# A two-layer graph network on one core: the order of the prelude's loads and checks, and the last tile's gelus and the first norms between two gather passes

## The chip, the cores and the metric

The kernel runs on one core of a Trainium2 chip. The core has TensorE (PE) for matrix products, VectorE (DVE), ScalarE (ACT), GpSimd (POOL) and SyncE (SP); SP, ACT and POOL each have a queue of their own for issuing DMAs. The metric is the device time of one execution in microseconds, the median of the runs.

## The reference

There are 3,125 nodes with 256 features, and 103,125 edges (`src`, `dst`, and one of eight types for each), sorted by `dst`, with one loop at each node. Cut to what matters:

```python
xn = layernorm(x)
e = relu((xn[dst] - xn[src]) @ theta.T + theta_b + xn[src] @ phi.T + phi_b)
x = x + segment_max(e, dst) + mixer(xn)              # layer 0: pass 0 over the edges
xt = layernorm(x)
x = x + layernorm(xt + ffn_two_of_eight_experts(xt))  # experts picked from the mean of xt
xn = layernorm(x)
h_all = einsum('ni,rio->nro', xn, W)                  # eight relation tables of 256
agg = segment_sum(h_all[src, type], dst)              # layer 1: pass 1 over the edges
x = x + layernorm(gelu(agg + xn @ loop_w + h_bias + xn)) + linear_attention(xn)
x = x + moe_ffn_two_of_eight(layernorm(x))
```

Since xn[dst] @ theta doesn't depend on the source, the maximum over a node's edges is a maximum over rows of one table of nodes, `xn @ (phi - theta)`.

## The kernel before

The nodes lie in 25 tiles of 128 rows (3,200 with padding). They are sorted by degree, so that all nodes of a tile have nearly as many edges; a tile's edges are then gathered column by column, 128 rows of 1 KB for each GpSimd indirect DMA.

*Prelude.* The lists `dst_i`, `src_i`, `typ_i`, `nxt_i` (`dst` moved by one) come as tiles of 124 partitions of 832 integers, all from ACT's queue, and behind them the two matrices `th0` and `w_b`. The node features `x` come from SP's queue. DVE, POOL and PE follow an order that is written out by hand (`tc.manual_schedule`); ACT and the queues of SP and ACT are ordered by a scheduler. The steps, in the order of the code:

- `blk_f` takes each block's first `dst`; four transposes on PE and copies on ACT spread it (`firsts`). `signs_of` (ACT) and `counts_of` (DVE, L1029) count for each node how many blocks begin before it; `stretches_of` makes addresses of that, and POOL gathers a stretch (`row`) of 496 entries for each of seven groups of tiles (`QUADS`).
- `idx2` is src times 8 plus type, written to `e_idx` in DRAM.
- `bad` holds the checks that the edges are sorted and looped as expected (seven DVE instructions, L1124 to L1133). With a check of degrees they give `flag`, by which all engines branch to a fast or a general form.
- `place_signs_of` (ACT) and `places_of` (DVE, L1059) count within the stretch; this gives where each node's edges end, and `edges_of` has POOL gather the node's edge list (`raw`) from `e_idx`.
- From the degrees come `key`, the one-hot `hot`, its running counts (`all_`, `own`, `cum`), and `rank`, each node's place in the sorted order.
- `node_stats` and `node_table` normalize five tiles of x at a time, transpose them and write their rows of `btab`, the node table of pass 0. `last_rows` finishes the last tile.
- `hi_oh` and `lo_oh` are one-hots of the rank's two parts. 25 products of them on PE give `in_i` and `id_i`, the nodes in sorted order.
- `ntab` in DRAM takes x, the edge list and the degree of each node. `fetch` gathers one tile's rows of it (`nrow`) in sorted order and makes the tile's gather addresses `idx1`, `idx2g`.

*Pass 0* gathers rows of `btab` (L183, buffers `gt`), takes maxima on DVE, and runs all other work of the layer (mixer, norms, expert products) beside it as background jobs. The experts are guessed beforehand from a part of the tiles; `settle` (run as `routing`) finds the real ones at the end.

*Between the passes.* The last group of tiles (tile 0) ends pass 0: `hidden_products`, then eight gelus on ACT (`hidden_gelus`, L1437), the output products (`outputs_a`) and copies (`outputs_out`). Then comes a branch on `missed`, taken if the guess was wrong (here it isn't). After it a class `Four` handles up to four tiles at once: `mixed` (sum and statistics on DVE, a square root on ACT), `added` (normalize on DVE, times gamma and plus beta on POOL), `summed` (sum into x, statistics, a square root on ACT), `normed`. `table` transposes the result, makes eight relation rows of it with 16 matmul records, scatters them to `htab_f` in sorted order from POOL (L230) and writes them to `here` from SP. The steps of the next group are spread over the tables of the one before. Tiles are cut so:

```python
cuts = ((23, 24), (24, 25), (21, 23), (1, 5), (5, 9), (9, 13), (13, 17), (17, 21), (0, 1))
```

*Pass 1* gathers from `htab_f` and runs the rest of layer 1 beside it.

Of the kernel before, what the change touches and what calls it, by code (L numbers as in the profile page):

```python
# [11 lines left out]
F32 = mybir.dt.float32  # L12
BF16 = mybir.dt.bfloat16
I32 = mybir.dt.int32
AF = mybir.ActivationFunctionType
ALU = mybir.AluOpType
AX = mybir.AxisListType
# [63 lines left out]
def gps_kernel(ctx: ExitStack, tc: tile.TileContext, a, out):  # L81
# [20 lines left out]

    xin = a["x"]
    V.memset(x[:, NT - 1, :], 0.0)
    for g in range(4):
        nc.sync.dma_start(
            x[:, 5 * g : 5 * g + 5, :],
            xin[5 * g * P : (5 * g + 5) * P, :].rearrange("(t p) d -> p t d", p=P),
        )
    nc.sync.dma_start(x[:, 20:24, :], xin[20 * P : 24 * P, :].rearrange("(t p) d -> p t d", p=P))  # L110
    nc.sync.dma_start(x[:LAST, NT - 1, :], xin[24 * P : NN, :])
# [816 lines left out]
    with ExitStack() as prx:  # L928
# [8 lines left out]
        def list_load(name, ap):  # L937
            t = pre.tile([LP, LT], I32, name=name)
            S.dma_start(t, ap.rearrange("(p t) o -> p (t o)", t=LT))
            return t  # L940
# [3 lines left out]
        typ_i = list_load("typ_i", a["typ"])  # L944
        nxt_i = list_load("nxt_i", a["dst"][1 : EPAD + 1, :])
        th0 = mat_load("th0", a["th_T"], pre, D)
        w_b = mat_load("w_b", a["ph_T"], pre, D)
# [127 lines left out]

        V.tensor_copy(blk_f, dst_i[:, ::BLOCK])
        for j in range(LT // BLOCK):
            pt = ps_tr.tile([P, 2, P], F32, name="pt")
            PE.transpose(pt[:, 0, :LP], blk_f[:, j : j + 1].to_broadcast([LP, P]), ident[:LP, :LP])
            S.copy(firsts[:, j * LP : (j + 1) * LP], pt[:, 0, :LP])  # L1080
# [7 lines left out]
        nc.sync.dma_start(e_idx.rearrange("r w -> (r w)")[W : W + EPAD].rearrange("(p t) -> p t", t=LT), idx2)  # L1088
        V.tensor_scalar(blk_n[:, 4:], blk_n[:, 4:], 0.5, 0.5 * NB, op0=ALU.mult, op1=ALU.add)
        stretches_of(slice(4, 7))  # L1090
        real = pre.tile([P, NT], F32, name="real")
        V.tensor_scalar(real, dval, float(NN), None, op0=ALU.is_lt)
        en = pre.tile([P, 29], F32, name="en")
        V.memset(en[:, 0:1], 0.0)
        V.tensor_scalar(rev, io_f[:, :W], -1.0, float(W - 1), op0=ALU.mult, op1=ALU.add)
        zero = pre.tile([2, W], F32, name="zero")
        V.memset(zero, 0)
        nc.sync.dma_start(e_idx[0:1, :], zero[0:1, :])
        nc.sync.dma_start(e_idx[EPAD // W + 1 :, :], zero[1:2, :])
        for s in fives:  # L1100
            nc.sync.dma_start(
                ntab[P * s.start : P * s.stop, :D].rearrange("(t p) d -> p t d", p=P), x[:, s, :]
            )
        prv_row = pre.tile([P, P], F32, name="prv_row")
        V.memset(prv_row[:, 0:1], 0.0)
        V.tensor_copy(prv_row[:, 1:], ident[:, : P - 1])
        prv_col = pre.tile([P, P], F32, name="prv_col")
        V.memset(prv_col, 0.0)
        V.tensor_copy(prv_col[:, 0:1], ident[:, P - 1 : P])
        ones_b = pre.tile([P, P], BF16, name="ones_b")  # L1110
        V.memset(ones_b, 1.0)
        not_upto = pre.tile([P, P], BF16, name="not_upto")
        V.tensor_scalar(not_upto, upto, -1.0, None, op0=ALU.add)
        one_f = pre.tile([P, NV * NT], BF16, name="one_f")
        V.memset(one_f, 1.0)
        floor = pre.tile([P, 1], F32, name="floor")
        V.tensor_scalar(floor, pcol, LAST - 0.5, -0.5, op0=ALU.is_lt, op1=ALU.add)
        V.tensor_scalar(floor, floor, 2 * BIG, None, op0=ALU.mult)

        for q in (1, 3, 5):  # L1120
            place_signs_of(q)

        bad = pre.tile([P, 3], F32, name="bad")
        V.memset(bad, 0.0)  # L1124
        big = pre.tile([LP, LT], F32, name="big")
        own_e = pre.tile([LP, LT], F32, name="own_e")
        V.tensor_tensor(big, dst_i, nxt_i, op=ALU.is_gt)
        V.reduce_sum(bad[:LP, 1:2], big, axis=AX.X)
        V.tensor_scalar(bad[:LP, 1:2], bad[:LP, 1:2], float(1 << 17), None, op0=ALU.mult)
        V.tensor_tensor(own_e, src_i, dst_i, op=ALU.is_equal)  # L1130
        V.tensor_tensor(big, nxt_i, dst_i, op=ALU.is_gt)
        V.scalar_tensor_tensor(big, own_e, -1.0, big, op0=ALU.mult, op1=ALU.mult)
        V.reduce_sum(bad[:LP, 2:3], big, axis=AX.X)  # L1133
# [30 lines left out]
        hot_1 = hot.rearrange("p v t -> p (v t)")  # L1164
        all_ = pre.tile([P, NV * NT], F32, name="all_")
# [8 lines left out]
        for g in (2, 3, 4):  # L1174
            node_stats(fives[g])
            last_rows = node_table(fives[g])

# [12 lines left out]
        V.tensor_scalar(rank, rank, -1.0, None, op0=ALU.add)  # L1190

# [16 lines left out]
        val = pre.tile(sh, F32, name="val")  # L1208
        V.tensor_tensor(val, hi_oh, dval[:, :, None].to_broadcast(sh), op=ALU.mult)
# [12 lines left out]
        pi = ps_mm.tile([P, 512], F32, name="mm")  # L1222
        for t in range(NT):
            if t == 2:
                V.reduce_sum(bad[:, 0:1], pc[:, :3], axis=AX.X)
                V.tensor_scalar(flag, bad[0:1, 0:1], float(NN), 1e6, op0=ALU.add, op1=ALU.min)
            lo_oh = pre.tile([P, P], F32, name="lo_oh", bufs=6)
            V.tensor_scalar(lo_oh, io_f, lo_f[:, t : t + 1], None, op0=ALU.is_equal)
            PE.matmul(pi[:, :NT], lo_oh, val[:, t, :], start=(t == 0), stop=(t == NT - 1))
        last_rows()  # L1230

        V.tensor_scalar(in_i, pi[:, :NT], float(NN - 1), None, op0=ALU.min)
        V.tensor_copy(id_i, pi[:, :NT])
# [4 lines left out]
    def fast():  # L1238
# [183 lines left out]
        def hidden_products(ts, i):  # L1422

            at0 = ts[0] * P
            ph = ps_mm.tile([P, 512], F32, name="mm")
            for f in range(FC):
                for c in range(2):
                    PE.matmul(
                        ph[:, f * P : (f + 1) * P], w1[:, i, c, f * P : (f + 1) * P], xT[:, c, at0 : at0 + P],
                        start=(c == 0), stop=(c == 1),  # L1430
                    )
            return ph
# [6 lines left out]
        def outputs_a(ts):  # L1439
            for j, t in enumerate(ts):  # L1440
                py = pys[t] = pys[t] if t in pys else ps_mm.tile([P, 512], F32, name="mm")
                PE.matmul(py, ones_row, b2.rearrange("o i d -> o (i d)"), start=True, stop=True)
                for i in range(2):
                    for f in range(FC):
                        PE.matmul(  # L1445
                            py[:, i * D : (i + 1) * D], hTs[i][:, f, j * P : (j + 1) * P], w2[:, i, f, :],
                            start=False, stop=(f == FC - 1), skip_group_check=True,
                        )

        def outputs_out(ts):  # L1450

            for t in ts:
                py = pys.pop(t)
                if t == 0:
                    y1 = seconds[t] = seconds[t] if t in seconds else f0h.tile([P, D], F32, name="y1_0", bufs=1)
                else:
                    y1 = seconds[t] = f0h.tile([P, D], F32, name="y1", bufs=SECONDS)
                S.copy(xT[:, :, t * P : (t + 1) * P], py[:, :D].rearrange("p (c n) -> p c n", c=2))
                S.copy(y1, py[:, D:])
# [21 lines left out]
        with ExitStack() as l0x:  # L1481
# [34 lines left out]
            fetch(2)  # L1516
# [264 lines left out]
            with tc.manual_schedule(engines={ET.DVE, ET.Pool, ET.PE, ET.Activation}):  # L1781
                fin[0].sums(0)
                fin[0].norms()
                routing = settle()
                next(routing)
                ts = GROUPS[-1]
                phs = [hidden_products(ts, i) for i in range(2)]
                for _ in routing:
                    pass
                for i in range(2):  # L1790
                    hidden_gelus(ts, i, phs[i])
                outputs_a(ts)
                outputs_out(ts)

        again = nc.values_load(missed[0:1, 0:1])
        with tc.If(again > 0):
# [8 lines left out]
            for ts in GROUPS:  # L1805
# [9 lines left out]
                hidden(ts)  # L1815
                outputs_a(ts)
                outputs_out(ts)
                if ts != GROUPS[-1]:
                    outputs_b(ts)
# [4 lines left out]
        with ExitStack() as tx:  # L1824
# [88 lines left out]
            cuts = ((23, 24), (24, 25), (21, 23), (1, 5), (5, 9), (9, 13), (13, 17), (17, 21), (0, 1))  # L1913
            fours = [Four(range(a, b)) for a, b in cuts]
            for part_ in fours[0].steps():
                for job in part_:
                    job()
            for four, after in zip(fours, fours[1:] + [None]):
                steps = after.steps() if after is not None else []
                each = -(-len(steps) // four.k)  # L1920
# [472 lines left out]
```

## Time and profile before

| | |
|---|---|
| median of 3 runs | 2603.63 us (2600.09 to 2603.84) |
| profiled execution | 2603.32 us, its span 2601.6 us |
| PE, DVE, ACT, POOL busy | 1792, 1263, 561, 1772 us |
| mean granted TensorE clock | 0.83 |
| prelude, to the first gather of pass 0 | 0 to 111.8 us |
| pass 0, first to last gather | 111.8 to 1184.4 us |
| between the passes, to the first gather from `htab_f` | to 1433.9 us |
| pass 1 and the end | to 2601.6 us |

The first three rows give the time and one execution's parts; times within the profile count from the start of its span. A row of the timeline that is shown further on gives the start in us, the duration in us (of all instructions of the row together), the engine, the line of the code, the operation, what it writes and reads, and in brackets how long the engine had been idle before and what released it. ACTq and SPq are the issues of DMAs on those engines. In the names buffer numbers are left out, so `idx` is `idx2` at L1087 and `idx1` in the gathers of pass 0.

### The profile page before, as it was taken

To read this page: it belongs to the slowest core of one execution; us is meant where nothing else is said; L and a number is where in the kernel's file an instruction comes from. 1 tells how busy PE (TensorE), PEld (TensorE's weight loads), DVE (VectorE), ACT (ScalarE), POOL (GpSimd) and SP (SyncE) were. 2 spreads that over 40 slices of the span, in tenths; PEclk is the share of its full clock that TensorE was granted. 3 is DMA by queue.
4 is the path that set the end of the run, shared out by engine and by line. 5 is a ranking of instruction groups with operands and counts; after the bars stand their busy time and mean duration, and the time that the engine had idled before them with its cause. 6 is when DMAs were issued, how large, how long until landed. Compare 5 with 4: busy or idle time off the path is not lost.

```text
span 2601.6 us, 20970 instructions
## 1 busy us (share of the span) xinstructions
PE 1792.2 (69%) x6143; PEld 1072.0 (41%) x6143; DVE 1262.6 (49%) x3108; ACT 561.0 (22%) x1319; POOL 1772.0 (68%) x1850
## 2 busy tenths in 40 slices
PE   1646677306743623764897627597898989999998
PEld 1523344104422312442343416243343545766787
DVE  6654656337344343444653344543635464655542
ACT  3313331002110100121121312121212122333333
POOL 3577777777777777772443777777776777777760
PEclk9777888657967767876999859698899989999998
DMA  6533334334333333331677753333333333333330
GB/s 181 126 107 108 105 104 122 103 103 133 102 103 103 103 101 103 103 102 59 248 299 304 224 155 102 111 100 105 97 103 89 103 108 107 102 106 101 103 90 13
DMA packets 128464, 314.99 MB, mean 121 GB/s; under 512 B 38636, under 2 KB 63282, under 8 KB 121932
## 3 DMA queue, kind: packets, MB, share of 16 engines
q0 software_dynamic: 86784, 252.90, 32.9%
q1 hardware_dynamic: 36510, 56.37, 6.4%
q10 hardware_dynamic: 5038, 4.21, 0.6%
q8 instruction: 53, 0.87, 0.1%
q14 instruction: 79, 0.65, 0.1%
HBM read 246.65 MB, written 66.70 MB: 120 GB/s over the span
## 4 chain that ended last, share of the span: by engine, by line
PE 26%; POOL 9%; issue 8%; DVE 5%; DMA 4%; ACT 1%; DVEq 0%; POOLq 0%; ACTq 0%
POOL gt L183 9%; PE mm L2156 8%; PE py L2189 8%; PE mm L178 7%; DMA gt<-htab_f,idx2g 3%; DVE gt L1269 1%; PE pt L2166 1%; PE mm L2050 1%; PE mm L2125 1%; DVE bnst L152 1%; DMA htab_f<-hs,id_i 1%; DVE hT L2174 0%; DMA out_dram<-x,id_i 0%; DVE acc L1274 0%; DMA xn<-here,own_i 0%
## 5 line engine op out<-in xcount | busy, mean ns | idle before, releaser
L183 POOL DMA_INDIRECT gt<-htab_f,idx2g x814 | 800.2, 983 | 269.4 <-issue 219.3
L183 POOL DMA_INDIRECT gt<-btab,idx x814 | 796.9, 979 | 251.6 <-issue 221.5
L1269 DVE TENSOR_TENSOR gt<-gt 128x256 f32<-128x256 f32 (+1 forms) x831 | 445.5, 536 | 738.8 <-DMA gt<-btab,idx 477.3
L2189 PE MATMUL py<-hT,w 128*128 128x256 f32 (+4 forms) x1408 | 384.1, 431 | 49.9 <-DVE hT L2174 49.9
L2156 PE MATMUL mm<-xT,w 128*128 128x256 f32 (+4 forms) x1408 | 375.0, 419 | 12.7 <-DVE x L2056 10.3
L2189 PEld LDWEIGHTS py<-hT,w 128*128 128x128 f32 x1408 | 245.7, 202 | 183.8 <-issue 81.2
L2156 PEld LDWEIGHTS mm<-xT,w 128*128 128x128 f32 x1408 | 241.6, 199 | 137.9 <-issue 86.0
L2160 ACT ACTIVATE hT<-mm,b 128x256 f32<-128x256 f32 (+4 forms) x352 | 170.3, 495 | 413.1 <-PE mm L2156 404.4
L178 PE MATMUL pt<-w_own,xT 128*128 128x256 f32 x100 | 37.4, 504 | 262.7 <-DVE acc L1685 262.7
L2174 DVE TENSOR_TENSOR hT<-hT,pt 128x1024 f32<-128x1024 f32 (+4 forms) x88 | 117.5, 1335 | 169.8 <-PE pt L2166 169.8
L178 PE MATMUL mm<-w_rel,xT 128*128 128x512 f32 x400 | 180.1, 609 | 4.4 <-ACT xT L173 3.6
L1274 DVE TENSOR_TENSOR acc<-acc,gt 128x256 f32<-128x256 f32 x403 | 172.7, 429 | 13.9
L178 PEld LDWEIGHTS pt<-w_own,xT 128*128 128x128 f32 x100 | 22.9, 254 | 273.5 <-DVE acc L1685 267.7
L178 PEld LDWEIGHTS mm<-w_rel,xT 128*128 128x128 f32 x400 | 76.6, 195 | 99.9 <-issue 85.8
L1416 PE MATMUL mm<-xT,w 128*128 128x384 f32 (+2 forms) x320 | 95.6, 464 | 14.9 <-DMA w<-in_f_W_dram 14.9
L1702 PE MATMUL pmean<-ones,xt 128*128 128x1 f32 (+1 forms) x100 | 21.7, 321 | 121.2 <-DVE xt L161 121.2
L1692 ACT ACTIVATE rs<-rs 128x3 f32<-128x3 f32 (+2 forms) x11 | 2.2, 204 | 452.4 <-DVE rs L1691 452.4
L1445 PE MATMUL mm<-w,hT 128*128 128x256 f32 x400 | 93.0, 386 | 0.1
L230 POOL DMA_INDIRECT htab_f<-hs,id_i x25 | 24.8, 990 | 96.9 <-DMA htab_f<-hs,id_i 25.3
L178 PE MATMUL mm<-w_qkv,xT 128*128 128x512 f32 (+1 forms) x200 | 87.2, 553 | 0.5 <-ACT xT L173 0.5
L1445 PEld LDWEIGHTS mm<-w,hT 128*128 128x128 f32 x400 | 74.1, 190 | 28.1 <-issue 18.2
L1416 PEld LDWEIGHTS mm<-xT,w 128*128 128x128 f32 x320 | 63.6, 219 | 46.3 <-DMA w<-in_f_W_dram 15.3
(398 smaller groups left out, 2143.6 us busy)
## 6 DMA issues: line engine op xcount, KB each, us to landing
here<-hs SPq DMA_DIRECT2D x25, 1024.0 KB, 3.9
gt<-btab,idx POOLq DMA_INDIRECT x814, 2.8
gt<-htab_f,idx2g POOLq DMA_INDIRECT x814, 2.8
w<-in_f_W_dram SPq DMA_DIRECT2D x20, 512.0 KB, 9.3
ntab<-x SPq DMA_DIRECT2D x5, 640.0 KB, 10.2
btab<-bs SPq DMA_DIRECT2D x5, 640.0 KB, 3.9
otab<-xn SPq DMA_DIRECT2D x25, 128.0 KB, 1.7
acc<-otab SPq DMA_DIRECT2D x25, 128.0 KB, 2.2
```

The source lines that it names most:

```text
L152: V.bn_stats(out=st, in_=src)
L178: PE.matmul(ps, lhs[:, c, t * P : (t + 1) * P], w[:, c, :], start=start and c == 0, stop=stop and c == 1)
L183: G.indirect_dma_start(out=dst, out_offset=None, in_=table, in_offset=bass.IndirectOffsetOnAxis(ap=idx, axis=0))
L1269: V.tensor_tensor(gt[:, :h, :], gt[:, :h, :], gt[:, m - h : m, :], op=op)
L1274: V.tensor_tensor(acc, own(t) if i == 0 else acc, gt[:, 0, :], op=op)
L1416: PE.matmul(ph[:, :n], w1[:, i, c, f * P : (f + 1) * P], xT[:, c, at0 : at0 + n], start=(c == 0), stop=(c == 1),)
L1445: PE.matmul(py[:, i * D : (i + 1) * D], hTs[i][:, f, j * P : (j + 1) * P], w2[:, i, f, :], start=False, stop=(f == FC - 1), skip_group_che ...
L2050: PE.matmul(pa, ones_row, b_lu, start=False, stop=True)
L2156: PE.matmul(ph[:, :n], w1s[e][:, c, f * P : (f + 1) * P], xT[:, c, at0 : at0 + n], start=(c == 0), stop=(c == 1),)
L2160: S.activation(hT[:, f, :n], ph[:, :n], AF.Gelu, bias=b1[:, e, f : f + 1])
L2174: V.tensor_tensor(hT[:, :, :n], hT[:, :, :n], wb[:, None, :n].to_broadcast([P, FC, n]), op=ALU.mult)
L2189: PE.matmul(self.py[c][:, :n], w2s[e][:, f, c * P : (c + 1) * P], hT[:, f, :n], start=False, stop=(e == NX - 1 and f == FC - 1),)
```

## The change

In the prelude, the lists, x and the matrices are loaded in one written order from SP's queue; the writes to `e_idx` go to ACT's queue; small set-up operations move ahead; the checks `bad` move behind `hot`; `last_rows` moves ahead to behind `rank`; `in_i` is found from two bf16 digits of the node's number; and the `fits` to `flag` part moves behind `in_i`. One tile is fetched in full before the first gather, and the second only asked for. Between the passes, the last tile's gelus and outputs move from before the branch to after the first steps of two groups, and the cuts change.

```diff
-            S.dma_start(t, ap.rearrange("(p t) o -> p (t o)", t=LT))
+            nc.sync.dma_start(t, ap.rearrange("(p t) o -> p (t o)", t=LT))
             return t
 
         dst_i = list_load("dst_i", a["dst"][:EPAD, :])
         src_i = list_load("src_i", a["src"])
         typ_i = list_load("typ_i", a["typ"])
+        V.memset(x[:, NT - 1, :], 0.0)
+        node_load(slice(0, 5))
+        th0 = mat_load("th0", a["th_T"], pre, D, nc.sync)
+        w_b = mat_load("w_b", a["ph_T"], pre, D, nc.sync)
+        node_load(slice(5, 10))
         nxt_i = list_load("nxt_i", a["dst"][1 : EPAD + 1, :])
-        th0 = mat_load("th0", a["th_T"], pre, D)
-        w_b = mat_load("w_b", a["ph_T"], pre, D)
+        node_load(slice(10, 15))
+        node_load(slice(15, 20))
+        node_load(slice(20, 24))
+        nc.sync.dma_start(x[:LAST, NT - 1, :], a["x"][24 * P : NN, :])
...
-        nc.sync.dma_start(e_idx.rearrange("r w -> (r w)")[W : W + EPAD].rearrange("(p t) -> p t", t=LT), idx2)
+        S.dma_start(e_idx.rearrange("r w -> (r w)")[W : W + EPAD].rearrange("(p t) -> p t", t=LT), idx2)
...
         V.reduce_sum(rank, cum.rearrange("p (v t) -> p t v", t=NT), axis=AX.X)
         V.tensor_scalar(rank, rank, -1.0, None, op0=ALU.add)
+
+        last_rows()
...
-        val = pre.tile(sh, F32, name="val")
-        V.tensor_tensor(val, hi_oh, dval[:, :, None].to_broadcast(sh), op=ALU.mult)
+        vals = pre.tile([P, NT, 2, NT], BF16, name="vals")
+        for m in range(2):
+            V.tensor_tensor(vals[:, :, m, :], hi_oh, digits[:, m, :, None].to_broadcast(sh), op=ALU.mult)
+        pi = ps_mm.tile([P, 512], F32, name="mm")
+        for t in range(NT):
+            lo_oh = pre.tile([P, P], BF16, name="lo_oh", bufs=6)
+            V.tensor_scalar(lo_oh, io128, lo_f[:, t : t + 1], None, op0=ALU.is_equal)
+            PE.matmul(pi[:, : 2 * NT], lo_oh, vals[:, t, :, :].rearrange("p m t -> p (m t)"), start=(t == 0), stop=(t == NT - 1))
+        id_f = pre.tile([P, NT], F32, name="id_f")
+        V.tensor_copy(id_f, pi[:, NT : 2 * NT])
+        V.scalar_tensor_tensor(id_f, pi[:, :NT], 64.0, id_f, op0=ALU.mult, op1=ALU.add)
+        V.tensor_scalar(in_i, id_f, float(NN - 1), None, op0=ALU.min)
+        V.tensor_copy(id_i, id_f)
...
-        pi = ps_mm.tile([P, 512], F32, name="mm")
-        for t in range(NT):
-            if t == 2:
-                V.reduce_sum(bad[:, 0:1], pc[:, :3], axis=AX.X)
-                V.tensor_scalar(flag, bad[0:1, 0:1], float(NN), 1e6, op0=ALU.add, op1=ALU.min)
-            lo_oh = pre.tile([P, P], F32, name="lo_oh", bufs=6)
-            V.tensor_scalar(lo_oh, io_f, lo_f[:, t : t + 1], None, op0=ALU.is_equal)
-            PE.matmul(pi[:, :NT], lo_oh, val[:, t, :], start=(t == 0), stop=(t == NT - 1))
-        last_rows()
-
-        V.tensor_scalar(in_i, pi[:, :NT], float(NN - 1), None, op0=ALU.min)
-        V.tensor_copy(id_i, pi[:, :NT])
+        V.reduce_sum(bad[:, 0:1], pc[:, :3], axis=AX.X)
+        V.tensor_scalar(flag, bad[0:1, 0:1], float(NN), 1e6, op0=ALU.add, op1=ALU.min)
...
-            fetch(2)
+            ask(2)
+            fetch(1)
...
                 for _ in routing:
                     pass
-                for i in range(2):
-                    hidden_gelus(ts, i, phs[i])
-                outputs_a(ts)
-                outputs_out(ts)
...
-            cuts = ((23, 24), (24, 25), (21, 23), (1, 5), (5, 9), (9, 13), (13, 17), (17, 21), (0, 1))
+            cuts = ((23, 25), (20, 23), (1, 5), (5, 9), (9, 13), (13, 17), (17, 20), (0, 1))
             fours = [Four(range(a, b)) for a, b in cuts]
-            for part_ in fours[0].steps():
+
+            first, second = fours[0].steps(), fours[1].steps()
+            for part_ in (first[0], second[0], first[1], second[1], first[2], first[3]):
                 for job in part_:
                     job()
+            for i in range(2):
+                hidden_gelus(GROUPS[-1], i, phs[i])
+            outputs_a(GROUPS[-1])
+            outputs_out(GROUPS[-1])
             for four, after in zip(fours, fours[1:] + [None]):
                 steps = after.steps() if after is not None else []
+                if four is fours[0]:
+                    steps = second[2:]
```

Not shown: the seven lines of `bad` are the same at their new place; so are the set-up operations; the five writes `ntab<-x` stand behind the node tables in the code, and in the order of SP's queue behind all loads and ahead of the first write of `btab`. The digits are the node's number shifted right by six and its low six bits. The second half of the expert outputs of tile 0 has no buffer of its own any more (`y1_0`); in the branch that isn't taken here, the last group redoes its hidden products only. The orders within both passes are the same as before. In the scheduled order of ACT after the branch stand: four gelus, the square root of tiles 23 and 24, one gelu, that of tiles 20 to 22, three gelus, a copy of the outputs, and the square root of 23 and 24 in `summed`.

## The prediction

> **What bounds the kernel now.** I read busy time by stage first, then the rows of DVE and POOL up to the first gather of pass 0, then ACT, PE and POOL between the passes. A row of the first view gives a stretch in us and its length, busy us (instructions) of PE, PE's weight loads, DVE, ACT and POOL, the granted clock, the DMA share and GB/s.
>
> ```profile
> 0.00:112.00 112.00, 47.15 (x218) 38.03 (x218) 71.15 (x223) 47.91 (x125) 41.04 (x75) 0.87 0.58 148
> 112.00:1186.00 1074.00, 563.52 (x1822) 342.03 (x1822) 499.66 (x1285) 169.99 (x489) 818.67 (x837) 0.73 0.38 108
> 1186.00:1434.00 248.00, 203.63 (x514) 95.65 (x515) 124.66 (x342) 47.39 (x111) 85.12 (x99) 0.91 0.62 238
> ```
>
> The reader is to see that pass 0 (row 2) is POOL's: 837 gathers in 1074 us, each 0.95 busy and 0.30 issue. The prelude (row 1) and the stretch between the passes (row 3) have no engine full, save PE at 82% in the latter. The change edits only these two, 360 us; the orders of instructions inside both passes stay. So the answer is how much earlier each pass's first gather starts.
>
> The prelude is a chain of waits. DVE:
>
> ```profile
> 12.04 0.17 DVE L1076 CAST blk_f<-dst_i 124x4 f32<-124x4 int32 x1 [8.57 <-DMA dst_i<-in_dst_dram]
> ...
> 24.48 1.03 DVE L1087 SCALAR_TENSOR_TENSOR idx<-src_i,typ_i 124x832 f32<-124x832 int32 x1 [0.69 <-DMA typ_i<-in_typ_dram]
> ...
> 32.35 1.03 DVE L1127 TENSOR_TENSOR big<-dst_i,nxt_i 124x832 f32<-124x832 int32 x1 [3.25 <-DMA nxt_i<-in_dst_dram]
> ...
> 41.99 0.72 DVE L1059 TENSOR_SCALAR_CACHE_REDUCE junk<-row,dval 128x496 bf16<-128x496 int32 x1
> ...
> 94.59 0.14 DVE L1226 TENSOR_SCALAR flag<-bad 1x1 int32<-1x1 f32 x1
> ...
> 105.10 0.18 DVE L1232 TENSOR_SCALAR in_i<-mm 128x25 int32<-128x25 f32 x1 [1.88 <-PE mm L1229]
> ```
>
> DVE waits for lists at 12.0, 24.5 and 32.4; the counting of places (L1059) starts at 42.0 only because the checks of the edges and the first statistics stand before it; the branch's `flag` is ready 10.5 us before the node order `in_i`, so the branch is hidden. What is released then, on POOL:
>
> ```profile
> 105.55 0.94 POOL L183 DMA_INDIRECT nrow<-ntab,in_i  x1 [16.54 <-DVE id_i L1233]
> ...
> 111.83 0.96 POOL L183 DMA_INDIRECT gt<-btab,idx  x1 [3.90 <-ACT x L1513]
> ```
>
> Between the passes, ACT leaves the branch at 1209.76, and PE gets its tables in starts and stops:
>
> ```profile
> 1209.76 1.28 ACT L1849 ACT_TABLE_LOAD   x1 [2.80 <-ACTq L1796]
> 1216.07 0.66 PE L172 MATMUL pt<-ident,z 128*128 128x128 f32 x2 [9.79 <-DVE z L161]
> 1217.19 8.76 PE L178 MATMUL mm<-w_rel,xT 128*128 128x512 f32 x16 [0.46 <-ACT xT L173]
> 1227.87 0.44 PE L172 MATMUL pt<-ident,z 128*128 128x128 f32 x2 [1.92 <-DVE z L161]
> 1228.77 7.13 PE L178 MATMUL mm<-w_rel,xT 128*128 128x512 f32 x16 [0.46 <-ACT xT L173]
> 1240.96 1.08 PE L172 MATMUL pt<-ident,z 128*128 128x128 f32 x4 [5.06 <-DVE z L161]
> 1242.07 15.13 PE L178 MATMUL mm<-w_rel,xT 128*128 128x512 f32 x32
> ```
>
> One tile's 16 records take 7.3 us; tiles 23, 24 and 21/22 each wait for norms that were begun too late. From 1260.7 on PE runs without a gap. The scatters (L230) stand at 1228.1, 1240.6, 1257.6, 1263.3, and then 21 intervals, 163.4 us in all, to 1426.7; the first gather from the table is at 1433.85.
>
> **The prelude, step by step.** *Loads.* The lists went out on ACT's queue beside x on SP's. Their 3,328-byte packets passed at 13 to 17 per us while x ran, at 24 when x paused (22 to 24 us); 124 packets are 5.2 us alone. Now dst, src, typ, x's first five tiles, th0 and w_b stand in that order in one queue: dst at 2.5 (first packets) + 5.2 + 0.5 = 8.2, src 13.4, typ 18.6, the x tiles 20.5, w_b some 22. Here a rule speaks against the change. The Trainium skill, "DMA: Bandwidth & Descriptors", section "Issuing engines are not separate DMA queues", says that transfers share the same 16 engines whoever starts them, so several issuers save only issue time; read so, one queue changes nothing for dst (12.0), the firsts gain only ACT's own delay, the prelude would gain some 8 us, and the time be 2586. I take the rows: the packets did slow down beside x, and a queue orders what two queues mix.
>
> *Firsts.* ACT issued six loads and started its first table load (1.28) at 17.5, so the firsts ended at 20.1; now they end at 11.3. Seven row gathers (1.25 each) follow, hidden behind DVE's wait for typ: idx2 runs 18.7 to 19.7, node_stats 20.6 to 23.4, the w_b subtraction (0.69), places at 24.3 against 42.0: -17.7. The small set-up operations that moved lie in the waits for lists.
>
> *To `hot`.* The first five tiles' table now shares ACT with the place signs; a product of the degree stands behind it on PE: +2.1. `hot` ends at 47.2 against 62.8. The checks (seven operations, 6.2 us by L1127 to L1133) come here, before node_table(1): 53.4. Its first xT follows at 55.2 against 66.82: -11.6. From there the five-tile groups and the scan keep their pace (ACT some 1.09 us a tile): rank 77.6 against 89.2.
>
> *Order.* From rank to in_i before: 15.9 us (val 0.81, fits to bad 2.4, 25 one-hots of 0.36, PE's tail 1.9). Now: a wait for the last tile's product to 80.5 (last_rows stands first), then 3.6 us to the end of two digit products (0.81 each), 25 one-hots, which become bf16, at 0.18 (a 128x128 bf16 output, L1113, took 0.16; at the old 0.36 it would be 4.5 more), 25 bf16 products instead of 50 fp32 records of 0.22, and three short operations: in_i at 89.5, 11.9 us.
>
> *Flag.* It now comes last: 3.6 us of DVE and PE, 93.1. Then every engine's branch, which nothing hides any more. Before shows ACT issuing 3.2 us after flag, and at the later branch DVE after 1.0 and ACT after 2.8; for POOL it shows only an upper bound, 10.9 us (flag to nrow). I take 2.1, between DVE's and ACT's. nrow at 95.2: -10.3. One tile is fetched before the first gather instead of two: 4.3 us instead of 6.3. First gather 99.5 against 111.8: **-12** (7 if the branch costs POOL 7, 17 if the lists land at 4.1 us each and the branch costs 1).
>
> *Costed at nothing:* the write of e_idx, moved to ACT's queue, holds ACT until idx2 and a load have come, near 22; behind it stand the place signs, whose rows don't land before 21 to 23. It lands about 31, and the 25 raw gathers (1.25 each) run to some 68 instead of 89; only the nrow gathers at 95 want them. ntab and the node table move past each other on SP: ntab's five writes (3.2 MB, some 14 us at 230 GB/s) follow the last x load, which lands near 34, and end near 48; the first node-table write behind them must free its buffer for group 2 at 63.5, so 13 us cover it.
>
> **Between the passes.** The last tile's gelus leave the stretch before the branch, where they lay beside it: ACT goes to the branch at 1202.3 instead of 1207.0, and is through at 1205.3. But ACT's order there is now four gelus, sqrt, one gelu, sqrt, three gelus, a copy, sqrt: six table loads in place of one after the branch and one before it, 7.7 us. Following it: sqrt of 23/24 at 1209.1, sqrt of the next three at 1212.2, copy 1215.3, sqrt 1216.8, norm, transposes, first table at 1218.2, 1.0 later than before. The Trainium skill, "ScalarE: Activation LUTs", section "What ACT_TABLE_LOAD costs", puts a switch at 2.66 us, 1.28 of load and 1.38 of drain. By that the six cost 8.3 more and this part would bring 1 us. The trace has the exponential done at 1200.82, the load at 1200.84 for 1.28, the gelu at 1202.13, so no drain; I take 1.28.
>
> Then the five tiles stand ready together. Scatters after the first table: +10.9, +18.3, +31 (four tiles' multiplies on POOL, 1.55 us each, stand before the third), +36.7, against +10.9, +23.4, +40.4, +46.1. The 21 intervals after it are bound by PE and the 1 MB writes as before, less 0.7 for one lone tile fewer. So -9.4 + 1.0 - 0.7: **-9** (5 to 13). The second buffer y1 and the rare branch cost nothing: not taken, or an allocation.
>
> **Sum.** The profiled execution took 2603.3 (span 2601.6), within 0.3 of the median of 2603.6. 2603.3 - 12 - 9 = 2582.
>
> **The rivals.** (a) *Half is eaten.* POOL's branch costs up to its bound of 10.9 and the prelude brings 3; or the scatters are bound by their writes from the first on, so that an earlier table start brings 2. For it: scatters wait for DMA in the dense part at 7.5 us each. Against it: the first four lie 12.5 and 17 apart, with idle PE. 2591 to 2595. (b) *No gain.* Both of these at once, or the skill's table switch with the branch at its bound: 2599 to 2603. (c) *Slower:* SP's one queue. All loads, ntab's writes and the node table's now stand in it in turn, and lists use few of the 16 engines. If that backlog frees the node-table buffer after 63.5, each us goes one for one into rank and the first gather. It takes back the whole gain at 84.5 and decides from 90 on (0.2%): the loads and writes would have to take 87 us in place of some 50. At 95 it gives 2613. For it: ACT waited for a node-table write already (0.7 us at 87.85). Against it: DMA is at 58% in the prelude, raw gathers move few bytes.
>
> **How the numbers follow.** 0.2% is 5.2 us, about what a measurement of this kernel can tell from no change. Both gains as summed: 0.70 (2574 to 2592, time 2582). (a) 0.13, (b) 0.07, (c) 0.10. Faster 0.83, same 0.07, slower 0.10. The range 2569 to 2599 takes in the low ends of the bounds (-17 and -13 together give 2573) and all of (a); (c) and most of (b) are left out.
>
> **What would show it.** Right: blk_f near 8, idx2 near 19 waiting for typ_i, the first place count near 24, hot before 50, nrow near 95 with POOL's wait named after flag or the branch, first gather 98 to 101; after the branch six table loads of 1.28, first table 1217 to 1220, five tiles with no gap, the first gather of pass 1 some 21 us earlier; pass 0 from first gather to last (1073 us) and pass 1 to the end (1168) as before. Wrong: a place count after 35, a node-table wait over 5 us, a drain beside the table loads, or either pass longer by more than 5.

## The result, and the profile after

The changed kernel takes 2590.8 us (median of 4 runs, 2588.7 to 2593.9) against 2603.7 us (4 runs): ratio 0.9952, 95% interval 0.9935 to 0.9969. It is 12.9 us faster; 2582 was forecast. The profiled execution, the slowest of the four, took 2593.92 us; its span of 2592.2 us is 9.4 us less than that of before. The windows, in the order of columns told above:

```profile
0.00:112.00 112.00, 46.73 (x193) 33.62 (x193) 69.64 (x227) 47.47 (x125) 43.87 (x75) 0.84 0.55 153
112.00:1186.00 1074.00, 571.86 (x1822) 345.58 (x1822) 498.80 (x1288) 170.26 (x489) 818.22 (x836) 0.73 0.37 107
1186.00:1426.00 240.00, 204.57 (x515) 96.53 (x516) 124.76 (x338) 52.66 (x114) 85.66 (x99) 0.91 0.64 246
```

The stretch between the passes is 8 us shorter with the same work in it; the prelude is as long as it was. By the starts of the gathers:

| stretch, us | before | after | change | forecast |
|---|---|---|---|---|
| to the first gather of pass 0 | 111.83 | 110.80 | -1.0 | -12 |
| pass 0, first to last gather | 1072.6 | 1073.0 | +0.4 | 0 |
| last gather to the first from `htab_f` | 249.4 | 241.8 | -7.7 | -9 |
| from there to the end | 1167.8 | 1166.7 | -1.1 | 0 |

In the prelude, DVE's rows (lines are numbered anew) show the gain being made:

```profile
9.59 0.17 DVE L1098 CAST blk_f<-dst_i 124x4 f32<-124x4 int32 x1 [5.39 <-DMA dst_i<-in_dst_dram]
...
19.95 1.03 DVE L1119 SCALAR_TENSOR_TENSOR idx<-src_i,typ_i 124x832 f32<-124x832 int32 x1 [3.84 <-DMA typ_i<-in_typ_dram]
...
25.05 0.72 DVE L1060 TENSOR_SCALAR_CACHE_REDUCE junk<-row,dval 128x496 bf16<-128x496 int32 x1
...
91.62 0.18 DVE L1230 TENSOR_SCALAR in_i<-id_f 128x25 int32<-128x25 f32 x1
...
95.05 0.14 DVE L1245 TENSOR_SCALAR flag<-bad 1x1 int32<-1x1 f32 x1
```

The place counts start 17 us earlier and `in_i` is ready 13.5 us earlier. POOL's rows show where those went:

```profile
104.76 0.95 POOL L173 DMA_INDIRECT nrow<-ntab,in_i  x1 [28.04 <-DMA wr<-in_f_WrT_dram]
...
110.80 0.96 POOL L173 DMA_INDIRECT gt<-btab,idx  x1 [3.65 <-issue]
```

`nrow` comes 13.0 us after the order that it needs. 3.4 of that is the flag, which now comes last; the other 9.6, from 95.19 on, are POOL's way through the branch. In the kernel before, flag was ready at 94.73; with the same 9.6 POOL would have been ready at 104.3, just before `in_i` at 105.3. By this estimate the branch was hidden there with 1 us to spare (3 us with 7.6 us, the shortest of the cases below), and a faster `in_i` alone could bring no more than that.

Between the passes, ACT's rows show the six table loads:

```profile
1205.95 1.28 ACT L1449 ACT_TABLE_LOAD   x1 [5.82 <-PEq L1802]
1207.25 1.14 ACT L1449 ACTIVATE hT<-mm,b 128x128 f32<-128x128 f32 x4
1208.41 1.28 ACT L1858 ACT_TABLE_LOAD   x1
1209.70 0.20 ACT L1858 ACTIVATE rsz<-rsz 128x2 f32<-128x2 f32 x1
1209.92 1.28 ACT L1449 ACT_TABLE_LOAD   x1
1211.22 0.37 ACT L1449 ACTIVATE hT<-mm,b 128x128 f32<-128x128 f32 x1
1211.61 1.28 ACT L1858 ACT_TABLE_LOAD   x1
1212.90 0.20 ACT L1858 ACTIVATE rsz<-rsz 128x3 f32<-128x3 f32 x1
```

and PE's rows the tables, back to back once they start:

```profile
1220.67 15.13 PE L168 MATMUL mm<-w_rel,xT 128*128 128x512 f32 x32
1235.64 0.60 PE L162 MATMUL pt<-ident,z 128*128 128x128 f32 x4
1236.48 14.00 PE L168 MATMUL mm<-w_rel,xT 128*128 128x512 f32 x32 [0.24 <-ACT xT L163]
```

The first table starts 36.9 us after the last gather of pass 0 instead of 32.8, but tiles 23, 24, 20 and 21 follow without a stop, and the fourth scatter stands at 72.8 instead of 78.8.

### The profile page after: what moved, and what is told of

It is laid out like the page before. It is cut to its first block, busy times and chain, and to the rows that moved or that the text cites. A ratio compares the mean times of both kernels' runs of the same rounds, so it can differ in the third digit from the quotient of the medians.

```text
span 2592.2 us, 20939 instructions
## 1 busy us (share of the span) xinstructions
PE 1805.1 (70%) x6118; PEld 1073.4 (41%) x6118; DVE 1261.3 (49%) x3111; ACT 566.6 (22%) x1321; POOL 1772.4 (68%) x1850
## 3 DMA queue, kind: packets, MB, share of 16 engines
q0 software_dynamic: 86784, 252.90, 32.8%
## 4 chain that ended last, share of the span: by engine, by line
PE 27%; POOL 8%; issue 7%; DVE 6%; DMA 4%; ACT 2%; DVEq 0%; POOLq 0%; ACTq 0%
PE mm L2173 8%; PE mm L168 8%; POOL gt L173 8%; PE py L2206 7%; DMA gt<-htab_f,idx2g 3%; DVE gt L1281 2%; PE pt L2183 1%; PE mm L2067 1%; PE mm L2142 1%; DVE acc L1286 1%; DVE bnst L142 1%; DVE hT L2191 0%; DMA out_dram<-x,id_i 0%; PE pt L2135 0%; ACT L2177 0%
## 5 line engine op out<-in xcount | busy, mean ns | idle before, releaser
L2206 PEld LDWEIGHTS py<-hT,w 128*128 128x128 f32 x1408 | 245.7, 202 | 181.5 <-issue 82.2
```

The lines of the kernel that those rows point to most:

```text
L2206: PE.matmul(self.py[c][:, :n], w2s[e][:, f, c * P : (c + 1) * P], hT[:, f, :n], start=False, stop=(e == NX - 1 and f == FC - 1),)
```

## The experiments

Each experiment had runs of the kernel before on the same chip; ratios are to those. Times within a kernel are from one profiled execution. Ratios and stretches both matter, because the stretch between the passes isn't the same in each execution of like code (see the last section).

**e1: flag ahead.** The lines from `fits` on move ahead of the digits, into DVE's wait for the last tile's product:

```diff
-        last_rows()
         r_i = pre.tile([P, NT], I32, name="r_i")
...
+        fits = pre.tile(sh, F32, name="fits")
...
+        PE.matmul(pc[:, :3], ones, bad, start=True, stop=True)
+        last_rows()
+        V.reduce_sum(bad[:, 0:1], pc[:, :3], axis=AX.X)
+        V.tensor_scalar(flag, bad[0:1, 0:1], float(NN), 1e6, op0=ALU.add, op1=ALU.min)
         vals = pre.tile([P, NT, 2, NT], BF16, name="vals")
```

> The changed kernel, with the part from fits to flag put ahead of the last tile's rows and of the digits, so that flag is ready some 6 us before the node order in_i instead of 3.4 us after it. Theory A (POOL pays about 9.6 us between flag and its first instruction of the branch, whatever it waits for besides): flag near 86, nrow 9 to 10 us later at 95 to 97, although in_i is ready near 93; first gather of pass 0 near 102 instead of 110.8, and the kernel some 8 to 9 us faster than the changed one. Theory B (the first nrow gather waits for the small load of wr that SP issues after the branch, as the profile names): nrow stays tied to the landing of that load, about 4 us after SP's issue of it. Theory C (in_i itself bound it): nrow within 1 us of in_i, near 93.

2580.8 us, ratio 0.9931 (0.9915 to 0.9948). DVE, then POOL:

```profile
85.98 0.14 DVE L1229 TENSOR_SCALAR flag<-bad 1x1 int32<-1x1 f32 x1
...
92.39 0.18 DVE L1243 TENSOR_SCALAR in_i<-id_f 128x25 int32<-128x25 f32 x1
```

```profile
93.94 0.94 POOL L173 DMA_INDIRECT nrow<-ntab,in_i  x1 [19.29 <-ACTq L2406]
...
101.19 0.96 POOL L173 DMA_INDIRECT gt<-btab,idx  x1 [4.87 <-issue]
```

`nrow` starts 7.8 us after flag and 1.4 after `in_i`: the branch is nearly hidden again, and the first gather is 9.6 us earlier, so the prelude has 10.6 of its 12 us. The 7.8 us are only an upper bound of what the branch cost here, since `nrow` had to wait for `in_i` too; they are less than theory A's 9 to 10. Theory B falls: SP begins to issue wr at 93.25, too late for a landing at 93.94. Theory C alone can't be right, since in the changed kernel `nrow` came 13.0 us after `in_i`.

**e9: the load of wr behind the others.** The two DMAs of `wr0` go behind the other loads of pass 0, since the profile names them as what POOL waited for.

> The changed kernel with the two loads of the small matrix wr moved behind the other loads of pass 0. Theory B (nrow waits for that load): nrow starts earlier, or moves to another load's landing. Theory A (the branch on POOL itself): nrow stays 9 to 10 us after flag, near 104.8.

One execution: flag at 94.20, `nrow` at 103.25, 9.1 us later. Counted from flag, SP issued wr 1.1 us later than in the changed kernel, and POOL went on 0.5 us earlier. With e1, where POOL goes on before wr can have landed, this shows that the releaser that the profile names is not the cause.

**e3: the late flag alone.** In the kernel before, only the lines from `fits` to `flag` move behind `id_i`.

> The kernel before with only one thing changed: the part from fits to flag stands behind in_i and id_i instead of ahead of the one-hots. in_i comes some 2.5 us earlier, near 102.5, flag near 106. Theory A (9.6 us from flag to nrow on POOL): nrow near 115.5, first gather near 121.5, the kernel about 10 us slower, ratio near 1.004. The value that the prediction took, 2.1 us: nrow near 108, first gather near 114, 2 to 3 us slower, within the noise.

2608.0 us, ratio 1.0024 (1.0015 to 1.0033): slower. DVE's flag, then POOL:

```profile
106.49 0.14 DVE L1233 TENSOR_SCALAR flag<-bad 1x1 int32<-1x1 f32 x1
```

```profile
115.16 0.94 POOL L183 DMA_INDIRECT nrow<-ntab,in_i  x1 [25.76 <-DMA br<-in_f_br_dram]
...
121.21 0.96 POOL L183 DMA_INDIRECT gt<-btab,idx  x1 [3.68 <-issue]
```

Flag was ready at 106.63, so POOL took 8.5 us, near theory A's 9.6, with another load named. The first gather is 9.4 us later than in before; over the whole kernel the ratio makes it 6 us.

**e10 to e13: the arms exchanged.** What goes on in those 8 to 10 us shows in the transfers. Ahead of flag nothing moves from 88 to 95 us; then, in the changed kernel, 95 to 104 us (queue, kind: packets, MB, share):

```profile
q14 instruction: 8, 0.07, 2.5%
q8 instruction: 2, 0.03, 1.6%
```

These are instructions being loaded: five packets start 1.5 to 1.7 us after flag and five more at 4.7 to 5.5 us. The trace doesn't say which engine each is for, and the last is in by 6.1 us; what fills the time until POOL goes on isn't shown. The fast form is the `Else` arm, which every engine has to jump to over the general form. The Trainium skill has this in "Runtime: NRT & Kernel Launch", section "Instruction fetch mechanics": a taken branch to a target outside the window already loaded stops the engine until its instructions are fetched. It gives no time. The test exchanges the arms:

```diff
-    with tc.If(unfit > 0) as branch:
-        general()
+    with tc.If(unfit < 1) as branch:
+        fast()
     with branch.Else():
-        fast()
+        general()
```

> The changed kernel with the two arms of the branch on flag exchanged: the fast form follows the branch directly, and the general one is jumped to. Nothing else is changed, flag stays last. Theory A in its narrow form (what POOL pays after flag is the jump: its next instructions have to be read anew, as the ten instruction packets after flag in the trace suggest): nrow starts 1 to 3 us after flag instead of 9.7, near 96 to 98, the first gather near 103, the kernel 6 to 8 us faster than the changed one, ratio to before near 0.992. Rival (the price lies in the reading of flag and the branch itself, or in waits of the first instruction): nrow stays 8 to 10 us after flag. At the end of the fast form there is now a jump over the general one; it may cost a few us at the end.

> The kernel of e10 once more, because in that call every kernel, the one before too, took 3,080 to 3,100 us. At the usual 2,600 us: flag near 95, nrow 2.9 us after it as in e10, near 98, the first gather near 104 instead of 110.8, and the kernel some 6.5 us faster than the changed one, ratio to before 0.992 to 0.994. If the jump is only moved to the end, the stretch from the last gather of pass 1 to the end is longer by as much, and the ratio 0.995.

On the chip of e10 and e11 every kernel, the one before too, took some 3,080 to 3,100 us, at a granted clock of 0.76 instead of 0.83, so both were run again on another chip as e12 and e13. DVE's flag, then POOL, in e12:

```profile
93.80 0.14 DVE L1245 TENSOR_SCALAR flag<-bad 1x1 int32<-1x1 f32 x1
```

```profile
96.69 0.94 POOL L173 DMA_INDIRECT nrow<-ntab,in_i  x1 [21.23 <-SPq L2406]
...
103.31 1.16 POOL L173 DMA_INDIRECT gt<-btab,idx  x1 [4.23 <-DVE idx L1521]
```

It is 2.75 us from flag to `nrow` instead of 9.6 (2.75 in e10 too), and no instruction packet is among the transfers from 94 to 103 us. So 6.8 of the 9.6 us go with the jump. But the whole kernel shows no clear gain by it: 2590.95 us, ratio 0.9956 (0.9938 to 0.9974), where 0.992 to 0.994 was expected; e10's ratio was 0.9931 (0.9895 to 0.9967), an interval that takes in both. In the profile of e12 the stretch between the passes is 246.0 us (241.8 in the changed kernel) and the rest 1168.3 (1166.7), which together give 5.9 of the 7.5 back.

Some of that is a jump again, now at the end of the fast form. POOL's last DMA in the changed kernel, whose span is 2592.2 us, then in e12, with 2589.4 us:

```profile
2584.69 0.96 POOL L220 DMA_INDIRECT out_dram<-x,id_i  x1 [42.12 <-DVE x L2231]
```

```profile
2579.76 0.96 POOL L220 DMA_INDIRECT out_dram<-x,id_i  x1 [42.11 <-DVE x L2231]
```

From its end to the end of the span it is 6.6 us in every kernel with the arms in the old order, and 8.5 to 8.7 us in the four with the arms exchanged; in e12 eight instruction packets come from 2579.5 to 2583.5 us, in the changed kernel none does so late. So some 2 us of the jump are paid there. Whether the layout of the arms lengthens the stretch between the passes too, or the spread of that stretch does, was not settled; with intervals this wide, a net gain of some 5 us could hardly be told from none.

> Both: flag put ahead as in e1, and the arms exchanged. If the price is the jump, the branch is hidden wholly: nrow within 0.5 us of in_i, near 93, which is 1 us earlier than in e1, and the first gather near 100; little more than e1, ratio to before 0.992 to 0.9935. If a jump at the end costs some us, no better than e1.

> The kernel of e11 once more, for the same reason. flag near 86, in_i near 92.6, nrow 1 us after in_i, the first gather near 100; ratio to before 0.991 to 0.993, 1 to 2 us less than e1.

e11 0.9954 (0.9926 to 0.9982); e13 2584.6 us, 0.9938 (0.9916 to 0.996). `nrow` is 1.0 us after `in_i` in both, with no jump in the way, so of the 1.4 us in e1 the jump holds at most 0.4. The first gather is at 97.7 in e13, the earliest of all, yet it isn't faster than e1, and its stretch between the passes is 245.7.

**e6: the loads undone.** The lists, th0 and w_b go back to ACT's queue, x beside them on SP's; the rest is the changed kernel, with the writes of `e_idx` still on ACT.

> The changed kernel with only the loads undone: the four lists and behind them th0 and w_b from ACT's queue, x from SP's queue beside them, as in the kernel before. Theory of the one queue: blk_f back at 12 us instead of 9.6, the copies of the firsts behind ACT's issues at 18 to 20, idx2 at 24 to 25, and w_b (behind four lists) holds DVE until 38 or later, so that the place counts start near 39 to 41 instead of 25.05 and the first gather of pass 0 comes 13 to 16 us later than 110.8. Rival (the queue only saves issue time): the place counts start 3 to 8 us later, the first gather 3 to 8 us.

2610.7 us, ratio 1.0031 (1.0017 to 1.0045). DVE's first place count and POOL's first gather:

```profile
40.03 0.73 DVE L1058 TENSOR_SCALAR_CACHE_REDUCE junk<-row,dval 128x496 bf16<-128x496 int32 x1 [3.00 <-DMA row<-in_dst_dram,blk_i]
```

```profile
128.01 0.96 POOL L173 DMA_INDIRECT gt<-btab,idx  x1 [2.84 <-issue]
```

The first gather comes 17.2 us later than in the changed kernel, a little more than the theory has it, but not by the way it gave: not w_b but the rows of `dst` held DVE. `dst_i` was there at 12.8 and ACT made the firsts only at 26.9, since it issued loads to 18.3 and the two small writes to `e_idx` at 24.6 before its first table load at 25.7. Some of the 17.2 is due to those writes, so this is not the loads' share alone. The list itself came 3.2 us later (9.59 in the changed kernel); most of the 15 us by which the place counts are later is ACT's delay.

**e2: the middle part alone.** The code behind the branch is that of the changed kernel, with `fetch(2)`; the prelude is that of before.

> The kernel before with only the part between the passes changed (gelus behind the first norms, new cuts, two groups up front); its prelude is that of before. If the parts add up: the last gather of pass 0 at 1184 as before, the first gather from htab_f 7 to 8.5 us earlier, near 1426, pass 1 as long as before within 2 us, ratio to before 0.9965 to 0.9975. If instead the gain of the whole change came from the prelude, or from a luckier pass 1, this shows a ratio of 0.999 to 1.001.

2596.4 us, ratio 0.9975 (0.9963 to 0.9987), some 6.5 us. The stretch is 244.3 us, 5.1 less than in before. The fourth scatter comes at 72.5 us after the last gather, as in the changed kernel.

**e4: the gelus back before the branch.** The changed kernel, with these lines at their old place (and the rare branch as in before):

```diff
                 for _ in routing:
                     pass
+                for i in range(2):
+                    hidden_gelus(ts, i, phs[i])
+                outputs_a(ts)
+                outputs_out(ts)
...
-            for i in range(2):
-                hidden_gelus(GROUPS[-1], i, phs[i])
-            outputs_a(GROUPS[-1])
-            outputs_out(GROUPS[-1])
             for four, after in zip(fours, fours[1:] + [None]):
```

> The changed kernel with the last tile's gelus and outputs back before the branch (as in the kernel before), the new cuts and the two groups up front kept. It splits the middle part into its two edits. Theory (the new cuts bring the gain, and the gelus behind the branch cost): ACT needs one table load after the branch instead of six; the first relation table starts some 33 us after the last gather of pass 0 instead of 36.9, and the first gather from htab_f comes 3 to 4 us earlier than in the changed kernel. Rival (the engines' start after the branch, not ACT's table loads, sets the first table): the first table starts 36 to 38 us after the last gather as in the changed kernel, and the stretch is as long within 1 us.

2594.0 us, ratio 0.9969 (0.9959 to 0.9979). The first table starts 35.2 us after the last gather, between the two theories, and the stretch is 240.1 us, 1.7 shorter than the changed kernel's. ACT after the branch:

```profile
1209.78 1.28 ACT L1862 ACT_TABLE_LOAD   x1 [2.48 <-ACTq L1809]
...
1217.75 0.21 ACT L1878 ACTIVATE rs<-rs 128x2 f32<-128x2 f32 x1 [6.38 <-DVE rs L1877]
```

There is one table load, at 1209.78 when the outputs are done; then DVE's norms of five tiles and POOL's multiplies set the time (the square root of `summed` waits 6.4 us for DVE). So the gelus' move costs 1.7 us in this stretch, if anything; the totals don't tell it from nothing. The gain is the cuts and the two groups normed together, which no run takes apart.

**e8: the gelus really behind the norms.** ACT's order is written out by hand and the gelus stand behind the tables of 23 and 24:

```diff
-            tx.enter_context(tc.manual_schedule(engines={mybir.EngineType.DVE, mybir.EngineType.Pool}))
+            tx.enter_context(
+                tc.manual_schedule(engines={mybir.EngineType.DVE, mybir.EngineType.Pool, mybir.EngineType.Activation})
+            )
...
+                if four is fours[1]:
+                    for i in range(2):
+                        hidden_gelus(GROUPS[-1], i, phs[i])
+                    outputs_a(GROUPS[-1])
+                    outputs_out(GROUPS[-1])
```

> The changed kernel with ACT's order between the passes written out by hand, and the gelus and outputs of the last tile put behind the tables of tiles 23 and 24, so that they really stand behind the first norms: three table loads in place of six. If the six table loads set the first table's start, it comes 33 to 34 us after the last gather instead of 36.9; but the output products, 4 us of PE that lay in idle time, now stand between tables, so the fourth scatter gains less than that, 0 to 2 us. If the start after the branch sets it, 36 to 38 us, and the fourth scatter is 2 to 4 us later than in the changed kernel.

2608.7 us, ratio 1.0029 (1.0013 to 1.0045): slower than before. PE:

```profile
1221.42 15.30 PE L168 MATMUL mm<-w_rel,xT 128*128 128x512 f32 x32
1236.66 1.12 PE L1454 MATMUL mm<-b,ones 1*128 1x512 f32 x2
1237.71 3.72 PE L1457 MATMUL mm<-w,hT 128*128 128x256 f32 x16
1241.27 0.60 PE L162 MATMUL pt<-ident,z 128*128 128x128 f32 x4
1242.44 7.13 PE L168 MATMUL mm<-w_rel,xT 128*128 128x512 f32 x16 [0.58 <-ACT xT L163]
```

With three table loads instead of six the first table starts at 35.7 us: the loads cost about 1 us there, not 3. (The seven kernels with six table loads that ran at the usual clock start it at 36.1 to 37.8 us; e4, e7 and e8 at 35.2 to 35.7.) The outputs of tile 0, which lay in PE's idle time, now stand between the tables (1236.7 to 1241.3), the fourth scatter comes at 76.8 instead of 72.8, and the 21 intervals after it take 167.8 us (161.5), with PE waiting 2.1 to 2.3 us for ACT's copies before six tables from 1275 to 1360 us. The stretch is 253.8 us. The 4 us at the fourth scatter fit the outputs' new place; the 6 us after it come with an order of ACT that is written out by hand for the whole stretch, so e8 doesn't show what the gelus' place alone is worth.

**e7: e1 and e4 together.**

> The changed kernel with flag put ahead (as in the run e1) and the gelus back before the branch. If both shifts add: first gather of pass 0 near 101, the middle stretch 3 us shorter than the changed kernel's, the kernel 11 to 13 us faster than the changed one, ratio to before 0.990 to 0.992. If only the flag counts: 0.993.

2583.9 us (2581.1 to 2587.1), ratio 0.994 (0.9923 to 0.9956), no better than e1. First gather 101.8, stretch 238.4 us. On the same chip e4, which differs from it only in the late flag, took 2594.0 us (2589.1 to 2598.6): flag ahead is worth some 10 us in total.

The lowest median is e1's, 2580.8 us, with e7 and e13 not to be told from it. It beats the kernel before; against the changed kernel the intervals (0.9915 to 0.9948 and 0.9935 to 0.9969) overlap a little, and it is e7 against e4 that shows the gain.

## Why the prediction was right, and where it was not

The direction and the range held (2569 to 2599), and both places were right; the size of one was not: 2582 was forecast and 2590.8 came. The range held because it was drawn to take in a costly branch; the sum itself was not right.

- *Loads and firsts:* `dst_i` 9.5 (8.2 forecast), idx2 19.95 (18.7), place counts 25.05 (24.3). Right. The order in one queue did count, as the slowed packets had it: `dst_i` came 2.5 us earlier than before, 3.2 earlier than in e6. But e6 has most of its delay from ACT, which issues loads and writes before it computes; that part the rejected reading, by which the firsts gain only ACT's own delay, had too.
- *To rank:* `hot` ended at 49.5 (47.2), as the degree's product waited 4.2 us, not 2.1; rank 81.4 (77.6). `in_i` 91.8 (89.5). Mostly right; 2.3 us of error. The raw gathers ran to 76.7, not 68, and as forecast cost nothing.
- *Flag:* 3.4 us after `in_i` (3.6). Right.
- *The branch:* taken at 2.1 us, measured 9.6. This is the step that failed: 7.5 of the 11.3 us by which the first gather came later than forecast. The prediction had a bound of 10.9 from POOL's own rows and chose a value by the other engines' rows, ACT's 3.2 and DVE's 1.0. Rival (a) named this very case, with 3 us for the prelude (1.0 came) and 2591 to 2595 as its time.
- *One fetch:* 6.0 us from `nrow` to the first gather (4.3). The row landed after 4.3 us (3.5 before), and POOL then sat 0.75 us. A gain of 0.2, not 2; it makes 1.7 of the 11.3.
- *Between the passes:* -7.7 (-9). The first table came 4.1 us later than before, not 1.0, though the table loads took 1.28 each and had no drain, as taken. e4 and e8 put 1 to 2 us of it on ACT's switches. The rest fits the longer norms: from the first square root to the table it is 11.0 us with five tiles (9.1 forecast) and was 6.1 with one. The scatters then came at +9.8, +16.4, +30.2 and +35.9 us from the first table (+10.9, +18.3, +31, +36.7), and the 21 intervals took 161.5 (163.4 before, 162.7 forecast).
- *Rival (c):* the writes of the node table held nothing up; the only loads or writes that DVE waited for in the prelude were `dst_i` (5.4 us) and `typ_i` (3.8), as forecast, and no wait of ACT for a write appears.

## What to carry to other kernels

A branch that an engine has to jump at is a piece of work with a price of its own; have its condition ready that much ahead of what follows, or let the usual arm stand directly behind it. Here the first was worth some 10 us; the second moved 2 us to the end and showed no clear gain in the whole kernel. When an idle engine's wait is shortened, ask what else was hidden in it: here a branch lay in POOL's wait with an estimated 1 to 3 us to spare. Where a cost has a bound from the engine's own rows, a value from another engine's rows is a guess.

## What the runs showed of the hardware that was not expected

- With an arm to jump over, POOL took 7.6 (e4) to 9.6 us (the changed kernel) from flag to its next DMA in the six kernels where flag came last; with the arms exchanged, 2.75, and 2 us more at the end. SP and ACT were through after 4.7 us in the changed kernel. The rows of e4:

```profile
94.94 0.14 DVE L1245 TENSOR_SCALAR flag<-bad 1x1 int32<-1x1 f32 x1
```

```profile
102.64 0.94 POOL L173 DMA_INDIRECT nrow<-ntab,in_i  x1 [28.00 <-DMA wr<-in_f_WrT_dram]
```

- The stretch between the passes spread from 234.6 us (e1) to 246.0 us (e12) with this stretch written alike. Most of it is the scatters' pace: the 21 intervals after the fourth took 153.0 us in e1 and 164.3 in e12, single ones 5.4 to 9.5 us. e1's profile is of the fastest of its four executions; the others with this stretch, at the usual clock, have 161.5 or more. What sets the pace was not found. The prelude spreads too: in e2, where it is that of before, the first gather comes at 114.15 instead of 111.83. So a few us in one profile, the prelude's -1.0 in the table among them, need not show in the medians.
